# Storing q and k unsplit in a graph-network kernel with attention: parting them later on GpSimd, with fewer loads per group and another order of the last gathers

## The chip, the cores and the metric

The kernel runs on one core of one Trainium2 chip. The metric is the device time of one execution in microseconds (us). Each kernel is run several times, and the median is taken.

## The reference

Four layers of a graph network work one after the other on x (3327 nodes, 128 features) with a sparse 0/1 matrix adj (3327 x 3327). Each layer normalises x, applies a ReLU and adds its result to x.

```python
def _L1_gnn_ref(x, adj, Wq, Wk, Wv, Wo):            # layer 1: attention, 128 heads of width 8
    q = (x @ Wq.T).reshape(d, n, h)                   # d = 128 heads, n = 3327, h = 8
    k = (x @ Wk.T).reshape(d, n, h)
    v = (x @ Wv.T).reshape(d, n, h)
    a = jnp.einsum('dnh,dmh->dnm', q, k) * scale
    a = jax.nn.softmax(a + adj + adj, axis=2)
    return jnp.einsum('dnm,dmh->dnh', a, v).reshape(n, h * d) @ Wo.T

def _L3_gnn_ref(x, A, W1, b1, W2, b2, sigma, k):      # layer 3: k = 4 nearest neighbours
    z = leaky_relu(_lap_mul(A, x) @ W1 + b1)
    S = exp(-sqrt(squared distances of z + 1e-10) / (2 * sigma))
    S = jnp.where(ranks < k, S, 0.0)                  # only the 4 largest of each row stay
    return _lap_mul(S + A, x) @ W2 + b2
```

Note the head: the reshape takes d first, so a head is a run of 3327 rows of 8 numbers in the flat list of all q (or k, or v). Layer 0 multiplies twice by adj, and layer 2 is a gated recurrent cell on adj @ x. They are not touched here.

## The kernel before, in words

Nodes are cut into T = 26 tiles of 128 rows. NH = 128 heads and E = 8 numbers per head are worked on in 32 groups of four heads. The queries are cut into seven chunks of QW = 476 columns (the last has 471), the keys into 26 tiles. So attention runs over chunk c, group g and key tile t: 7 x 32 x 26 steps.

**Projection (L399 to L425).** For each row tile r, TensorE makes q, k and v in PSUM. [...]q and k are parted here into a rounded half (hi, written by ScalarE, L410) and the rest (lo, L411, on VectorE). Both halves go to DRAM: `qt` and `kt` have HL = 16 rows, eight of hi and eight of lo, and a column for each node of each head. `store` (L395) issues three transfers per tile on SyncE's queue: q, k and v (with a column of ones for the softmax's sum, EA = 9). At r = 1 the loads of the first group are issued (L421), and half of its keys are cast.

**Loads of a group (`load_heads`, L347 to L367).** For each of four heads and two halves j: one load of 16 rows of k (hi and lo) into `k_in`, and two loads of 8 rows of q, the same half twice, so that a 32-row product gives (hi + lo) x (hi + lo). Then one load of v per head. That makes 28 transfers on SyncE's queue. They are issued at t = 4 of the group before. From t = 13 on, `key_pair` (L370 to L375) casts two key tiles per step from `k_in` into tiles of fp32r on GpSimd (L374).

**Attention (L523 to L562).** The order of instructions on each engine is that of the program here (a manual schedule). A step (`scores`, L481) multiplies keys and queries for four heads (L492). The doubled adjacency is added by VectorE (L497) for three or two heads (`early` tiles), or by TensorE with a diagonal matrix (L495, `late` tiles). ScalarE takes the exponential of the `late` ones (L498), GpSimd multiplies the last head of every odd step by exp of the doubled adjacency (L500), and at every odd step ScalarE takes the exponential of the five summed parts of two steps at once (L502). Four steps later `weigh` multiplies by v (L509) and, at the last key tile, copies the result out of PSUM (L518) and stores it to `ot` (four transfers, L521). At t = 22 a stripe of the adjacency of the next chunk is loaded (`a_in`, L173) and doubled on GpSimd (L272); stripes already doubled are stored as bf16 for later layers (L479).

**Tail (L630 on).** The degree's root and several scales are made (L652 to L655, `scales`), then a loop over 26 row tiles divides by the softmax's sum, transposes and multiplies by Wo (L656 to L678). In the last layer, after the four neighbours of each node are found, `gather` (L878 to L899) fetches three rows per node by indirect transfers on GpSimd's queue (L886), five tiles per batch in one buffer `rows`, while TensorE makes the product with the adjacency; VectorE weighs and sums the rows (L894 to L899), the first of its operations, L895, being the one that frees `rows`. After all batches the output stage (L904 to L914) transposes, scales, adds and stores.

A tile of memory with one buffer can only be filled again when all its readers are done; a transfer on SyncE's queue waits on SyncE itself, with everything behind it.

Of the kernel before, what the change touches and what calls it, by code (L numbers as in the profile page):

```python
# [21 lines left out]
P = 128  # L22
# [32 lines left out]
def kernel(  # L55
# [273 lines left out]

    kt = dpool.tile([HL, GP], F32, name="kt")  # L330
# [15 lines left out]

    def load_heads(c, g):  # L347
        q0, _ = q_chunks[c]
        we = even(c)
        k_in = kq.tile([P, NP], F32, name="k_in", bufs=1)  # L350
        q4 = kq.tile([P, QW], F32R, name="q4")
        v4 = kq.tile([P, 4, T, EA], F32, name="v4")
        for i in range(4):
            n0 = (4 * g + i) * N
            for j in range(2):
                r = 32 * i + HL * j
                nc.sync.dma_start(k_in[r : r + HL], kt[:, n0 : n0 + NP])
                for k in range(2):
                    nc.sync.dma_start(
                        q4[r + E * k : r + E * k + E, :we].bitcast(F32),  # L360
                        qt[E * j : E * j + E, n0 + q0 : n0 + q0 + we],
                    )
            nc.sync.dma_start(
                v4[:, i].rearrange("p t e -> p (t e)"),
                vd[n0 : n0 + NP, :].rearrange("(p t) e -> p (t e)", t=T),
            )
        return k_in, q4, v4, []  # L367
# [9 lines left out]
    with tc.tile_pool(name="l1", bufs=1) as pool, tc.tile_pool(name="l1_ps", bufs=3, space=PSUM) as ps:  # L377
# [6 lines left out]
        for tail in (qt, kt):  # L384
            nc.gpsimd.dma_start(tail[:, N * NH :], zero)
# [12 lines left out]
        assert 3 * N + NP <= P * NH  # L398
        for r in range(T):  # L399
            kp = rows_of(r)  # L400
            lhs = hT[:, r * P : r * P + kp]
            for i, (dst, mx) in enumerate(((qt, q_max), (kt, k_max))):
# [3 lines left out]
                scale = D**-0.5 if i == 0 else 1.0  # L406
                s = st.tile([P, 2, E * NH], F32R, name="qk_st")
                full = pp[:kp].rearrange("p a b -> p (a b)")
                hi = s[:kp, 0].bitcast(F32)
                nc.scalar.activation(s[:kp, 0], full, AF.Copy, scale=scale)  # L410
                nc.vector.scalar_tensor_tensor(s[:kp, 1], full, scale, hi, op0=ALU.mult, op1=ALU.subtract)  # L411
                nc.vector.tensor_reduce(mx[:kp, r : r + 1], hi, AX.X, ALU.max, apply_absolute_value=True)
                store(dst.rearrange("e (r c) -> r e c", c=NH), s.bitcast(F32).rearrange("p a (e c) -> p (a e) c", c=NH), r, kp)
# [7 lines left out]
            if r == 1:  # L421
                first = load_heads(0, 0)
                while len(first[3]) < T // 2:
                    key_pair(first)
                e_first = [exp_of(a, 0) for a in a_first[1::2]]  # L425
# [38 lines left out]
    with tc.tile_pool(name="at_in", bufs=2) as a_pool, tc.tile_pool(name="at_p", bufs=3) as p_pool, tc.tile_pool(  # L464
# [5 lines left out]
        def load_adj(c, t):  # L470

            q0, w = q_chunks[c]
            a = a_pool.tile([P, QW], F32, name="a_in")
            load_rows(a, adjT, t, q0, w)
            return doubled(adj_pools[c % 2], a[: rows_of(t), :w], t, w)
# [47 lines left out]
        with tc.manual_schedule(engines=engines):  # L523
# [7 lines left out]
            for j, step in enumerate(steps):  # L531
# [14 lines left out]
                if t == min(4, T // 2) and more:  # L546
                    coming = load_heads(*groups[n])

                if t >= T // 2 and more:
                    key_pair(coming)  # L550
                if t == max(T - 4, 0) and c + 1 < len(q_chunks):
                    for _ in range(min(len(to_store), 1 + T // n_groups)):
                        store_adj(*to_store.pop(0))
                    while len(a_next) < T * (g + 1) // n_groups:
                        to_store.append((c + 1, len(a_next), load_adj(c + 1, len(a_next))))
                        a_next.append(to_store[-1][2])
# [73 lines left out]
    def tail(general):  # L630
# [13 lines left out]
        with ExitStack() as s:  # L644
# [7 lines left out]
            d1 = inv_sqrt(pool, deg, "d1")  # L652
            d1_in, d1_out = d1, d1
            if not general:
                d1_in, d1_out, into4, back4 = scales(pool, d1)  # L655
            with tc.tile_pool(name="lo", bufs=3) as lo, tc.tile_pool(name="lo_ps", bufs=2, space=PSUM) as ps:  # L656
                wo_s = lo.tile([NH, E, D], F32, name="wo_s", bufs=1)
                nc.gpsimd.dma_start(wo_s, wo)
                for t in range(T):
# [18 lines left out]
                    done(t + 1)  # L678

# [195 lines left out]
            cuts = list(range(0, T - T % 5, 5)) + [T]  # L875
            near_0 = 0 if general else 1

            def gather(t):  # L878
                if t not in cuts[:-1]:
                    return  # L880
                p = slice(t, cuts[cuts.index(t) + 1])
                n = p.stop - p.start
                rows = gpool.tile([P, n, 4 - near_0, D], F32, name="rows")
                for i in range(n):
                    for k in range(near_0, 4):
                        nc.gpsimd.indirect_dma_start(  # L886
                            out=rows[:, i, k - near_0, :],
                            out_offset=None,
                            in_=yd,
                            in_offset=bass.IndirectOffsetOnAxis(ap=idx[:, t + i, k : k + 1], axis=0),  # L890
# [7 lines left out]
                nc.vector.tensor_mul(w[:, :, 0], w[:, :, 0], over_t(d2_out, t, n))  # L898
                nc.vector.tensor_add(xs[:, p], xs[:, p], w[:, :, 0])  # L899

            with tc.tile_pool(name="l3_g", bufs=1) as gpool:
                agg = new_agg(pool)
                adj_product(agg, y, parts, gather)
            with tc.tile_pool(name="l3_o", bufs=3) as opool, tc.tile_pool(name="l3_ops", bufs=3, space=PSUM) as ps:  # L904
                for t0, n in quads():
                    op = ps.tile([P, 4, D], F32, name="op")
                    for j in range(n):
                        nc.tensor.transpose(op[:, j, :], slots(agg)[:, t0 + j, :], ident)  # L908
                    o = opool.tile([P, 4, D], F32, name="o")
                    nc.vector.tensor_mul(o[:, :n], op[:, :n], over_t(d2_out, t0, n))  # L910
# [137 lines left out]
```

## Time and profile before

| | |
|---|---|
| time of three runs, median | 11345.91 us (11337.25 to 11353.99) |
| the profiled execution | 11325.28 us |
| its span, mean granted clock of TensorE | 11323.4 us, 0.987 |
| TensorE busy | 10928.7 us (97%) |
| ScalarE (ACT) busy | 10214.7 us (90%) |
| VectorE (DVE) busy | 9415.9 us (83%) |
| GpSimd (POOL) busy | 5706.9 us (50%) |
| first store of the projection, first ACT instruction of attention | 387.85 us, 645.44 us |
| last gather issued | 11287.96 us |

The profile is of one execution. A busy TensorE isn't at its peak, since its matmuls are pipelined and their ends are modelled. A line of a group reads: line, engine, operation, out<-in with shapes, count | busy us in all, mean ns of one | idle time of the engine just before them, and what ended most of it. In a timeline a line begins with its start and its duration in us, and the bracket gives the engine's idle time before it. "SPq" and "POOLq" are the queues on which SyncE and GpSimd issue transfers. A wait is put down to whichever release came last by the records.

### The profile page before, as it was taken

What the parts mean: (1) busy time and instruction counts of PE and PEld (TensorE: products, weight loads), DVE (VectorE), ACT (ScalarE), POOL (GpSimd) and SP (SyncE); (2) the same over time, 40 slices, a digit from 0 to 9 for tenths busy, and PEclk for the clock granted to TensorE, in tenths of its full rate; (3) what the DMA queues carried; (4) which work ended last, traced back from release to release, by engine and by line L of the source; (5) the groups of instructions that cost most, each with busy time, mean ns of one, the idle gap of its engine ahead of it and who ended that gap; (6) DMA issues with size and microseconds to landing.
All of it is one profiled execution on the core that took longest, in us unless ns stands there. A gap on an engine that the chain in (4) does not pass through costs nothing. (4 is left out here: it accounts for less than half of the span.)

```text
span 11323.4 us, 210681 instructions
## 1 busy us (share of the span) xinstructions
PE 10928.7 (97%) x79530; PEld 3042.0 (27%) x79530; DVE 9415.9 (83%) x15475; ACT 10214.7 (90%) x9152; POOL 5706.9 (50%) x6196
## 2 busy tenths in 40 slices
PE   9789999999999999999999999999999999999896
PEld 4322222222222222222222222222222222222453
DVE  8678888888888888888888888888888888888655
ACT  0379999999999999999999999999999999999532
POOL 0135555555555555555555555555555555555203
PEclk9899999999999999999999999999999999999998
DMA  7754444443444444444444444444444443434432
GB/s 265 243 128 62 65 68 61 65 66 61 69 63 63 68 62 66 66 61 68 63 65 67 61 65 66 60 69 63 62 68 60 67 61 55 62 54 60 139 104 96
DMA packets 475902, 888.06 MB, mean 78 GB/s; under 512 B 91472, under 2 KB 422721, under 8 KB 439292
## 3 DMA queue, kind: packets, MB, share of 16 engines
q1 hardware_dynamic: 471114, 864.70, 43.3%
q8 instruction: 629, 10.31, 0.5%
q0 software_dynamic: 3760, 9.79, 0.3%
q14 instruction: 399, 3.27, 0.1%
HBM read 761.66 MB, written 112.46 MB: 77 GB/s over the span
## 5 line engine op out<-in xcount | busy, mean ns | idle before, releaser
L497 DVE TENSOR_TENSOR p<-early,a 128x476 f32<-128x476 f32 (+1 forms) x14560 | 8441.8, 646 | 1408.1 <-PE early L492 1166.6
L502 ACT ACTIVATE p<-p 128x2380 f32<-128x2380 f32 (+1 forms) x2912 | 6785.7, 2330 | 13.7 <-DVE p L497 0.9
L509 PE MATMUL acc<-p,v 128*9 128x476 f32 (+1 forms) x46592 | 5872.0, 564 | 34.7 <-POOL p L500 14.2
L500 POOL TENSOR_TENSOR p<-p,e 128x476 f32<-128x476 f32 (+1 forms) x2912 | 3537.4, 1215 | 3301.0 <-ACT p L498 3243.5
L498 ACT ACTIVATE p<-late 128x476 f32<-128x476 f32 (+1 forms) x5824 | 4552.6, 907 | 40.4 <-DMA q<-qt 20.6
L492 PE MATMUL early<-q,k 32*128 32x476 f32 (+1 forms) x14560 | 2884.4, 477 | 19.0 <-DVE p L497 19.0
L492 PE MATMUL late<-q,k 32*128 32x476 f32 (+1 forms) x8736 | 2798.9, 478 | 62.1 <-ACT p L498 36.1
L374 POOL CAST k<-k_in 128x256 fp32r<-128x256 f32 x2912 | 1944.9, 702 | 1155.2 <-DMA q<-qt 581.7
L492 PEld LDWEIGHTS late<-q,k 32*128 32x128 f32 x8736 | 1066.8, 181 | 4767.3 <-ACT p L498 3235.9
L495 PE MATMUL late<-a,two_i 128*128 128x476 bf16 (+1 forms) x5824 | 2181.1, 374 | 0.0
L492 PEld LDWEIGHTS early<-q,k 32*128 32x128 f32 x14560 | 1147.1, 181 | 24.7 <-DVE p L497 19.7
L509 PEld LDWEIGHTS acc<-p,v 128*9 128x9 f32 x46592 | 710.7, 88 | 1400.1 <-issue 1184.5
L495 PEld LDWEIGHTS <-two_i 128*128 128x128 bf16 x5824 | 556.2, 96 | 1326.3 <-issue 1326.3
L189 ACT COPY agg<-agg_ps 128x512 f32<-128x512 f32 x15 | 8.2, 591 | 484.1 <-PE agg_ps L204 290.5
L230 PE MATMUL agg_ps<-a,part 128*128 128x512 bf16 (+1 forms) x1092 | 227.1, 369 | 3.6 <-ACT agg L861 3.2
L272 POOL TENSOR_SCALAR a<-a_in 128x476 bf16<-128x476 f32 (+2 forms) x156 | 222.4, 1425 | 0.5
L410 ACT ACTIVATE qk_st<-pp 128x1024 fp32r<-128x1024 f32 (+1 forms) x52 | 53.2, 1023 | 150.2 <-DMA qt<-qk_st 67.8
L856 PE MATMUL sp<-yT,hT 128*128 128x512 f32 (+1 forms) x364 | 171.1, 611 | 12.2 <-ACT agg L861 6.3
L272 POOL TENSOR_SCALAR a<-a 128x476 bf16<-128x476 f32 (+1 forms) x26 | 36.4, 1400 | 287.8 <-DMA a<-in_adjT_dram 287.8
L204 PE MATMUL agg_ps<-a,h 128*128 128x512 f32 (+2 forms) x364 | 148.1, 570 | 26.8 <-DVE h L164 26.8
L411 DVE SCALAR_TENSOR_TENSOR qk_st<-pp,qk_st 128x1024 fp32r<-128x1024 f32 (+1 forms) x52 | 63.7, 1224 | 122.7 <-ACT qk_st L410 122.5
L518 DVE COPY o<-acc 105x476 f32<-105x476 f32 (+1 forms) x224 | 144.4, 644 | 4.6 <-PE acc L509 4.6
(231 smaller groups left out, 2438.3 us busy)
## 6 DMA issues: line engine op xcount, KB each, us to landing
k_in<-kt SPq DMA_DIRECT2D x1792, 208.0 KB
v<-vd SPq DMA_DIRECT2D x896, 117.0 KB
a<-in_adjT_dram SPq DMA_DIRECT2D x50, 1663.5 KB
a<-adj SPq DMA_DIRECT2D x78, 831.8 KB
q<-qt SPq DMA_DIRECT2D x3072, 14.9 KB
a_in<-in_adjT_dram SPq DMA_DIRECT2D x125, 238.0 KB
qt<-qk_st SPq DMA_DIRECT2D x25, 1024.0 KB
kt<-qk_st SPq DMA_DIRECT2D x25, 1024.0 KB
```

Source lines behind the costliest of these rows:

```text
L204: nc.tensor.matmul(acc[c][:, :w], lhs[:kp, t, :], a[:kp, c0 : c0 + w], start=(t == 0), stop=(t == T - 1))
L230: nc.tensor.matmul(acc[c][:, :w], part[:, t, :], a[:, c0 : c0 + w], start=(t == 0 and i == 0), stop=(t == T - 1 and i == len(parts) - 1),)
L272: nc.gpsimd.tensor_scalar(a2[:kp, :w], a, 2.0, None, op0=ALU.mult)
L374: nc.gpsimd.tensor_copy(k, slots(k_in)[:, t : t + 2, :])
L492: nc.tensor.matmul(sp[:, :we], pairs[t // 2][r, t % 2, :], q4[r, :we], start=True, stop=ways[i] != "I")
L495: nc.tensor.matmul(late[:, i - n_d, :we], two_i, a2[:, :we], start=False, stop=True)
L497: nc.vector.tensor_tensor(p8[:, places[i], :we], early[i][:, :we], a2[:, :we], op=ALU.add)
L498: nc.scalar.activation(p8[:, places[n_d] : places[3] + 1, :we], late[:, :, :we], AF.Exp)
L500: nc.gpsimd.tensor_tensor(p8[:, places[3], :we], p8[:, places[3], :we], e_a[:, :we], op=ALU.mult)
L502: nc.scalar.activation(p8[:, :5, :we], p8[:, :5, :we], AF.Exp)
L509: nc.tensor.matmul(acc[32 * i : 32 * i + EA, :w], v4[:kp, i, t, :], p8[:kp, PLACES[t % 2][i], :w], start=(t == 0), stop=(t == T - 1),)
L856: nc.tensor.matmul(sp[:, c0 : c0 + w], slots(zT)[:, t, :], z2T[:, cols], start=True, stop=False)
```

## The change

It has six parts.

1. ScalarE copies q and k as they are (plain fp32) into one staging tile, and they are stored whole in new tensors `qf` and `kf`. L411 goes. A class `Parting` loads four heads' q or k from there as [96 x 1109] (8 numbers x 12 strips), makes hi with a cast and lo with a subtraction on GpSimd in four pieces of 278 columns, and stores both halves to `kt` or `qt`. Groups 0 and 1 are parted during the projection, each later group during chunk 0.
2. `load_heads` loads q with one transfer of 16 rows instead of two of 8, reading 8 rows twice; all k and q come before the four loads of v: 20 transfers per group. The columns beyond N are set to zero by GpSimd. The first group's loads move to where its halves have been stored.
3. In chunk 0 the parting of group g + 2 is spread over the steps: k in pieces at t = 2 to 5, q at t = 6 to 9, the four stores at t = 11, and the two loads for the group after it at t = 15.
4. The stripe of adjacency is loaded at t = 6 and doubled at t = 22; the pool of `a_in` and `o4` has one buffer.
5. The degree's root and the scales are made after the Wo loop.
6. Gathers are cut 5, 5, 5, 5, 4, 2; `rows` becomes two buffers (batches 0, 1, 2 and 4 use one, 3 and 5 the other), and the last three batches stand in the output stage's loop, between the output of the row tiles (in fours, a quad) that are already gathered. GpSimd issues, in the order built: batch 0, nine of batch 3, batch 1, the rest of batch 3, batch 2, batch 4, batch 5.

The general path (a fallback that isn't run with these inputs) is adapted, which is left out here.

```diff
+    JW = 12
+    WJ = 4 * N // JW
+    W4 = -(-WJ // 4)
+    SIDES = ((kf, kt, "lo_k"), (qf, qt, "lo_q"))
+    class Parting:
+        def __init__(self, g):
+            self.g, self.hi, self.lo = g, [None] * 2, [None] * 2
+        def rows(self, ap, r):
+            return dram(ap, r * GP + 4 * self.g * N, [[GP, E], [WJ, JW], [1, WJ]])
+        def load(self, side):
+            src, _, name = SIDES[side]
+            self.lo[side] = kq.tile([E * JW, WJ], F32R, name=name, bufs=1)
+            nc.sync.dma_start(self.lo[side].bitcast(F32), self.rows(src, 0))
+        def part(self, side, i):
+            if i == 0:
+                self.hi[side] = kq.tile([E * JW, WJ], F32R, name=f"hi{side}", bufs=1)
+            p = slice(i * W4, min((i + 1) * W4, WJ))
+            hi, lo = self.hi[side][:, p], self.lo[side][:, p]
+            nc.gpsimd.tensor_copy(hi, lo.bitcast(F32))
+            nc.gpsimd.tensor_sub(lo, lo.bitcast(F32), hi.bitcast(F32))
+        def store(self, side):
+            dst = SIDES[side][1]
+            nc.sync.dma_start(self.rows(dst, 0), self.hi[side].bitcast(F32))
+            nc.sync.dma_start(self.rows(dst, E), self.lo[side].bitcast(F32))
...
     def load_heads(c, g):
+        nc.gpsimd.memset(k_in[:, N:], 0.0)
+        if w % 2:
+            nc.gpsimd.memset(q4[:, w : w + 1].bitcast(F32), 0.0)
         for i in range(4):
             n0 = (4 * g + i) * N
             for j in range(2):
                 r = 32 * i + HL * j
-                nc.sync.dma_start(k_in[r : r + HL], kt[:, n0 : n0 + NP])
-                for k in range(2):
-                    nc.sync.dma_start(
-                        q4[r + E * k : r + E * k + E, :we].bitcast(F32),
-                        qt[E * j : E * j + E, n0 + q0 : n0 + q0 + we],
-                    )
+                nc.sync.dma_start(k_in[r : r + HL, :N], kt[:, n0 : n0 + N])
+                nc.sync.dma_start(q4[r : r + HL, :w].bitcast(F32), dram(qt, E * j * GP + n0 + q0, [[0, 2], [GP, E], [1, w]]))
+        for i in range(4):
+            n0 = (4 * g + i) * N
             nc.sync.dma_start(
...
+        early = []
+        for g in range(2):
+            part = Parting(g)
+            for side in range(2):
+                early.append(lambda part=part: (part.load(0), part.load(1)) if part.lo[0] is None else None)
+                early.append(lambda part=part, side=side: [part.part(side, i) for i in range(4)] and part.store(side))
+        first, e_first = [], []
+        early.append(lambda: first.extend(load_heads(0, 0)))
+        ahead_part = Parting(2)
+        early.append(lambda: (ahead_part.load(0), ahead_part.load(1)))
+        early.append(lambda: e_first.extend(exp_of(a, 0) for a in a_first[1::2]))
+        early += [lambda: (key_pair(first), key_pair(first))] * (T // 4)
...
         for r in range(T):
-                s = st.tile([P, 2, E * NH], F32R, name="qk_st")
-                full = pp[:kp].rearrange("p a b -> p (a b)")
-                hi = s[:kp, 0].bitcast(F32)
-                nc.scalar.activation(s[:kp, 0], full, AF.Copy, scale=scale)
-                nc.vector.scalar_tensor_tensor(s[:kp, 1], full, scale, hi, op0=ALU.mult, op1=ALU.subtract)
-                nc.vector.tensor_reduce(mx[:kp, r : r + 1], hi, AX.X, ALU.max, apply_absolute_value=True)
-                store(dst.rearrange("e (r c) -> r e c", c=NH), s.bitcast(F32).rearrange("p a (e c) -> p (a e) c", c=NH), r, kp)
+                s = st.tile([P, E * NH], F32, name="qk_st")
+                nc.scalar.activation(s[:kp], pp[:kp].rearrange("p a b -> p (a b)"), AF.Copy, scale=D**-0.5 if i == 0 else 1.0)
+                nc.vector.tensor_reduce(mx[:kp, r : r + 1], s[:kp], AX.X, ALU.max, apply_absolute_value=True)
+                store(dst[:E].rearrange("e (r c) -> r e c", c=NH), s.rearrange("p (e c) -> p e c", c=NH), r, kp)
...
-            if r == 1:
-                first = load_heads(0, 0)
-                while len(first[3]) < T // 2:
-                    key_pair(first)
-                e_first = [exp_of(a, 0) for a in a_first[1::2]]
+            if r > 1 and early:
+                early.pop(0)()
...
+                if c == 0 and g + 2 < n_groups:
+                    if t == 0:
+                        parting = ahead_part
+                    for due in range(t, t + 1 if t < T - 1 else max(T, 16)):
+                        parting.at(due)
+                        if due == 15 and g + 3 < n_groups:
+                            ahead_part = Parting(g + 3)
+                            ahead_part.load(0)
+                            ahead_part.load(1)
...
-                if t == max(T - 4, 0) and c + 1 < len(q_chunks):
+                if t == min(6, T // 2) and c + 1 < len(q_chunks):
                     for _ in range(min(len(to_store), 1 + T // n_groups)):
                         store_adj(*to_store.pop(0))
-                    while len(a_next) < T * (g + 1) // n_groups:
-                        to_store.append((c + 1, len(a_next), load_adj(c + 1, len(a_next))))
-                        a_next.append(to_store[-1][2])
+                    a_in = [load_adj(c + 1, i) for i in range(len(a_next), T * (g + 1) // n_groups)]
+                if t == max(T - 4, 3) and c + 1 < len(q_chunks):
+                    for a, i, w in a_in:
+                        a_next.append(doubled(adj_pools[(c + 1) % 2], a[: rows_of(i), :w], i, w))
+                        to_store.append((c + 1, i, a_next[-1]))
...
-            cuts = list(range(0, T - T % 5, 5)) + [T]
+            cuts = [c for c in (0, 5, 10, 15, 20, 24) if c < T] + [T]
...
+                turn = i % 2 if i > 2 else 0
+                rows = gpool.tile([P, n, 4 - near_0, D], F32, name=f"rows{turn}")
...
+            n_beside = min(3, len(batches))
             with tc.tile_pool(name="l3_g", bufs=1) as gpool:
                 agg = new_agg(pool)
-                adj_product(agg, y, parts, gather)
+                adj_product(agg, y, parts, lambda t: gather(cuts.index(t)) if t in cuts[:n_beside] else None)
+                with tc.tile_pool(name="l3_o", bufs=3) as opool, tc.tile_pool(name="l3_ops", bufs=3, space=PSUM) as ps:
+                    to_write = quads()
+                    for i in range(n_beside - 1, len(batches)):
+                        if i >= n_beside:
+                            gather(i)
+                        while to_write and sum(to_write[0]) <= batches[i].stop:
```

In `Parting.at`, side 0 (k) is parted at t = 2 to 5, side 1 (q) at t = 6 to 9, and both are stored at t = 11.

## The prediction

> **What bounds the kernel now.** I read the groups of the page first, then the busy time of three stretches (projection, attention, tail), then the waits of each and the timelines around them.
>
> ```profile
> L502 ACT ACTIVATE p<-p 128x2380 f32<-128x2380 f32 (+1 forms) x2912 | 6785.7, 2330 | 13.7 <-DVE p L497 0.9
> L500 POOL TENSOR_TENSOR p<-p,e 128x476 f32<-128x476 f32 (+1 forms) x2912 | 3537.4, 1215 | 3301.0 <-ACT p L498 3243.5
> L374 POOL CAST k<-k_in 128x256 fp32r<-128x256 f32 x2912 | 1944.9, 702 | 1155.2 <-DMA q<-qt 581.7
> ...
> 380.00:655.00 275.00, 175.44 (x353) 64.37 (x352) 131.80 (x130) 87.61 (x87) 18.95 (x42) 0.84 0.93 269
> 2060.00:3480.00 1420.00, 1404.81 (x10803) 349.44 (x10795) 1220.33 (x2109) 1415.19 (x1261) 793.54 (x857) 1.00 0.43 65
> 11200.00:11324.00 124.00, 26.57 (x132) 15.17 (x129) 38.64 (x41) 1.56 (x3) 59.20 (x56) 0.61 0.26 80
> ```
>
> The last three are stretches: length, busy PE, PEld, DVE, ACT, POOL (instructions), clock, DMA share, GB/s. In attention (645 to 10590 us) ACT is busy 99.7%: it sets the pace. In the projection nothing computes much and the DMA engines are 93% busy; in the tail POOL's gathers lead. So three stages, three limits.
>
> In attention, a pair of steps takes 3.367 us between the starts of undisturbed L502, 43.78 us for 13 pairs; the mean group takes 44.44. Most of the excess is in one place: from t=19 to t=21, L502 to L502 takes 3.77 us in the mean. One group:
>
> ```profile
> 2093.81 1.21 POOL L500 TENSOR_TENSOR p<-p,e 128x476 f32<-128x476 f32 x1 [2.18 <-ACT p L498]
> 2100.28 1.33 POOL L374 CAST k<-k_in 128x256 fp32r<-128x256 f32 x2 [5.26 <-DMA q<-qt]
> 2101.58 1.20 POOL L500 TENSOR_TENSOR p<-p,e 128x476 f32<-128x476 f32 x1
> ...
> 2102.07 1.74 PE L509 MATMUL acc<-p,v 128*9 128x476 f32 x8
> ...
> 2103.32 2.65 ACT L502 ACTIVATE p<-p 128x2380 f32<-128x2380 f32 x1
> ...
> 2107.31 2.19 ACT L502 ACTIVATE p<-p 128x2380 f32<-128x2380 f32 x1
> ```
>
> POOL stands 5.26 us at the key cast of t=13, because the 28 loads of the next heads aren't all in. The L500 behind it starts at 2101.58 where the rhythm asked for 2097.2, PE's L509 is stretched from about 0.98 to 1.74, and the next L502 starts 3.99 us after its predecessor, not 3.37. Medians over groups, counted from L502(t=1): cast due 21.9, started 27.0, last k landed 25.6, L500(15) 4.4 late, L502(21) 0.40 late. Hence L500 has some 4.05 us of slack, and 0.40 x 223 = 89 us hang on this one wait.
>
> The projection is bound by its stores:
>
> ```profile
> 575.06 1.17 SPq L395 DMA_DIRECT2D qt<-qk_st  x1
> 576.32 3.92 SPq L395 DMA_DIRECT2D kt<-qk_st  x1
> 580.34 3.53 SPq L395 DMA_DIRECT2D vd<-v_st  x1
> ...
> 645.44 0.57 ACT L498 ACTIVATE p<-late 128x476 f32<-128x476 f32 x1 [20.61 <-DMA q<-qt]
> ```
>
> A tile of 128 rows every 9.02 us, and attention begins only when every store has landed. From the first store (387.85) to 645.4 are 257.6 us.
>
> **What the Trainium skill says.** "DMA: Bandwidth & Descriptors", § Why a DMA increments its semaphore by 16 and not by 1: a transfer runs on the largest number of engines, up to 16, that divides the outermost size of both sides. The packets agree: four ot stores of 9 rows leave 36 packets of data and 36 four-byte packets, one from each engine used; q loads of 8 rows leave 8. "SBUF — State Buffer", § Who interferes with whom: GpSimd reading SBUF contends with a VectorE instruction that has two SBUF inputs, not with one input. L497 reads PSUM and one SBUF tile, and L500 keeps its 1215 ns beside it. "GPSIMD Engine Reference", § 3.1: two-input elementwise work costs about 2.6 cycles an element, 2.17 ns; here 3328 elements took 7.24 us, 2.18 ns each.
>
> **The change, part by part.** 1. *Whole q and k.* A tile's q and k were 4096 packets of 512 bytes at 26.9 ns over 16 engines, 6.9 us, and v 128 packets of 4608 bytes at 0.21 us, 1.7 us. Halving the first gives 3.45 + 1.7 = 5.15, at the old ratio of pace to sum (9.02/8.6) 5.4 us; 26 tiles 140 us instead of 234.5. L411 goes from DVE (52 x 1.22 us, already beside the stores); the compute pace is then an estimated 3.6 us (three ACT copies of about a microsecond), so stores still lead. Added before attention: 6 loads and 8 stores of 96 rows, whose DRAM side has outer size 8, so 8 engines with 12 packets of about 0.19 us: 14 x 2.3 = 32 us on engines 0 to 7. The head loads cost those engines some 8 (k) + 4 (v), and q, whose source now begins with a repeat of 2, runs on two engines: 8 packets of 0.1 us (an a_in load of this shape drains in about 0.8 us) x 8 = 6.4 on engines 0 and 1. Sum 191. Bubbles: SP waits for GpSimd's parts before the first kt store (about 6 us of parts per side, half of it behind queued stores), for stored rows before the head loads, and for the last landing: 14. So about 205 against 257.6: **−52** (−35 to −75: the upper end if the parting runs on all 16 engines). Behind the waiting SP stand the next tiles' stores, nothing of ACT's that isn't waiting for them already. POOL's 16 pieces hold up the v_st memsets by at most 12 us, which four staging buffers and the store queue cover; uncovered it costs about 6 a side.
>
> 2. *20 loads per group instead of 28.* k and q alternate over 8 lanes, v follows. Bytes of k are the same: a k load holds 16 engines 0.7 to 1.7 us, in the mean 1.4. On engines 0 and 1 I count 7 x (1.2 + 0.9) + 1.2, from the first packet 6.3 after L502(1): the last k lands near 22.5 to 23.5, cast 1 to 2 us late instead of 5.1. That is inside the slack of 4.05, so the stretched pair goes: **−85** of 89. If a q load costs 1.5 us on its two engines, k lands at 26 or later and nothing is won; if k alone counts, it lands at 18. What is late next: nothing on POOL; ACT's own floor. k_in's pad memset (one short strip) and the zero column of q4 are under 0.3 us on POOL, at t=4, where it idles 2.2 us a pair.
>
> 3. *Parting in chunk 0.* 30 groups x 8 pieces, each a cast and a subtraction of 96x278. Scaled to 278 columns, the cast row (0.702 for 256) gives 0.76 and the L500 row (1.215 for 476) 0.71, up to 0.82 where a part of it is fixed: a piece is 1.42 to 1.64; I take 1.52, 365 us of POOL in all, beside ACT. L500(9) follows seven pieces, three L500 and the memset: 1.2 + 7 x 1.52 + 3.6 + 0.3 = 15.8 after L500(1), due 13.5: 2.3 late (1.6 to 3.2), inside 4.05. By t=13 the idle 2.15 us per pair has taken it back. Queued behind POOL's pieces: L500, and through it L509; SP's four stores at t=11 wait for POOL, with the lo loads of t=15 and the next head loads of t=4 behind them: 10 steps of room. **0**, from 0 to +48 (a piece of 2.0 would lose 1.6 us a group). No gain is possible here: it is added work.
>
> 4. *a_in loaded at t=6, doubled at t=22.* L272 waited 0.5 us in all: 0. With one buffer the load waits for a doubling 10 steps older: 0. If that cover failed, one group would lose at most the 2 us of a transfer.
>
> 5. *d1 and the scales after the Wo loop.* They delay its start by 3 us through PE's queue; afterwards DVE does them beside the adjacency loads: **−3** (0 to −5).
>
> 6. *Gathers.* 78 issues, and before each later batch a wait for DVE:
>
> ```profile
> 11239.89 2.08 POOL L886 DMA_INDIRECT rows<-yd,idx  x1 [4.01 <-DVE w L895]
> 11264.51 2.08 POOL L886 DMA_INDIRECT rows<-yd,idx  x1 [4.14 <-DVE w L895]
> ```
>
> Four gaps were 5.02, 5.48, 4.01, 4.14 = 18.6 us; two row buffers in turn leave one of about 5: −13.6, given back by 3 to 5 of slower issues beside DVE (2.08 instead of 0.94, as above). The last batch has 2 tiles, DVE behind it 2.9 instead of 7 us: −3. The order of DVE's instructions keeps all output work behind the last batch, so the output isn't really written in between: 0. Together **−12** (−8 to −18).
>
> Sum: −52 −85 −3 −12 = −152. The profiled execution took 11325.28 us (span 11323.4), so 11173; it lies 20.6 under the median of 11345.91, which makes **11194** in the terms of the runs.
>
> **The rivals.** *A: the head loads stay late.* Half the transfers per q, but on two engines; the cast still starts after 26. For it: 8 of the 20 transfers get slower; against: k no longer shares the engines with v. Gain 52 + 3 + 12 and some 5: 11274. *B: POOL's pieces cost 1.85 to 2.05 us,* past the slack by 0.5 to 2 us a group in chunk 0, 15 to 60 us: about 11232. For it the one pair of shapes never timed; against it the two rows above. *C: SP held by POOL and by the 8-engine transfers eats the projection's gain,* 15 left of 52: 11231. *D, slower: the pieces on POOL pass ACT's pace in chunk 0.* Past the slack, each group loses 7p − 12.4 us; all 152 are lost at 5.1 a group, p = 2.5 us, that is 1.25 an instruction, more than a 476-column L500 takes now; at p = 2.8 11194 + 30 x 7.2 = 11410. For it only that a cast and a subtraction of this shape were never timed; against it L500's steadiness beside DVE. *E: nothing changes in attention and projection alike,* 11330: the packets halve by construction, so hardly.
>
> **How the numbers follow.** Forecast 0.56 (11150 to 11215), A 0.17 (11255 to 11290), B 0.12, C 0.09, D 0.04, E 0.02. The range for 8 in 10 runs from 11150 (the upper ends, 75 + 89 + 5 + 18 = 187, give 11159, and the runs of one kernel lie 8 us to either side) to 11278, which takes in B, C and most of A; left out are D, E, a part of A and what lies below. A measurement of this kernel tells 0.2% (23 us) from no change. Faster by over 0.2%: 0.56 + 0.17 + 0.12 + 0.09 = 0.94, less 0.01 of spill; within: 0.03; slower: 0.04.
>
> **What would show it.** Right: a tile's three stores every 5.4 us, attention's first ACT some 205 us after the first store; no POOL idle above 2 us before the cast at t=13; L502 from t=19 to t=21 back to 3.37; POOL's pieces at 0.7 to 0.8 us; one DVE wait among the gathers. Wrong: packets of q in a long train on few engines with the cast waiting on k; a wait of L509 for L500 at t=9 to 11 in chunk 0; SP standing at the kt stores with idle DMA engines; gathers slowed to 2 us throughout.

## The result, and the profile after

The changed kernel takes 11188.99 us in the median (11184.25 to 11195.14, 4 runs) against 11344.12 (11337.25 to 11353.99): the ratio is 0.9864, with a 95% interval of 0.9852 to 0.9876. The prediction, 11194 in a range from 11150 to 11278, holds it. Its sum doesn't hold term by term, though. The span of the profiled execution went from 11323.4 to 11193.4 us, 130 and not 152 less, and the parts are these:

| stretch | before | after | difference | predicted |
|---|---|---|---|---|
| start to first store | 387.85 | 386.04 | -1.8 | 0 |
| first store to first exponential of attention | 257.6 | 190.2 | -67.4 | -52 |
| attention, to the end of the last big exponential | 9942.8 | 9897.0 | -45.8 | -85 |
| from there to the end | 735.2 | 720.2 | -15.0 | -15 |

The medians differ by 155 us and the spans by 130, because the profiled execution of before (11325.28) lies 19 us under the median of its kernel, and that of the changed kernel (11195.14) 6 us over its own. So the total was met because two errors of the sum cancelled in part, and because of this difference. To that extent it's luck.

The groups of the changed kernel's page, then the busy time of three stretches (length, PE, PEld, DVE, ACT, POOL with instructions, clock, DMA share, GB/s):

```profile
L557 ACT ACTIVATE p<-p 128x2380 f32<-128x2380 f32 (+1 forms) x2912 | 7568.4, 2599 | 0.4
L555 POOL TENSOR_TENSOR p<-p,e 128x476 f32<-128x476 f32 (+1 forms) x2912 | 3528.1, 1212 | 3204.3 <-ACT p L553 2998.6
L419 POOL CAST k<-k_in 128x256 fp32r<-128x256 f32 x2912 | 1936.5, 697 | 886.4 <-DMA k_in<-kt 339.4
...
380.00:580.00 200.00, 155.70 (x332) 66.06 (x331) 69.63 (x70) 83.50 (x84) 34.66 (x73) 0.86 0.88 260
2060.00:3480.00 1420.00, 1402.89 (x10855) 344.85 (x10851) 1224.19 (x2120) 1420.00 (x1267) 799.75 (x893) 1.00 0.34 65
11075.00:11193.00 118.00, 35.72 (x176) 19.49 (x173) 46.81 (x53) 1.56 (x3) 64.70 (x59) 0.66 0.33 108
```

ACT is now busy for all of the 1420 us. The third line is the surprise: POOL still stands 886 us before the key casts, 270 less than before. So the loads of k are still late, and the prediction's sign "no POOL idle above 2 us before the cast at t=13" didn't come. What changed is whether anybody suffers from it. From the waits of TensorE, first before, then after:

```profile
PEld acc L509 <- POOL p L500: 132.7, 182, 1.7
```

```profile
PEld acc L564 <- POOL p L555: 8.9, 20, 1.1
```

The columns are microseconds in all, times, longest. The wait of the product with v for GpSimd's multiplication is nearly gone. In one group of the changed kernel:

```profile
2018.17 1.21 POOL L555 TENSOR_TENSOR p<-p,e 128x476 f32<-128x476 f32 x1 [2.17 <-ACT p L553]
2023.28 1.32 POOL L419 CAST k<-k_in 128x256 fp32r<-128x256 f32 x2 [3.89 <-DMA adj<-a]
2024.56 1.20 POOL L555 TENSOR_TENSOR p<-p,e 128x476 f32<-128x476 f32 x1
```

POOL stands 3.89 us, not 5.26, and L555 starts at 2024.56 where the rhythm asks for 2021.56: 3.0 late, inside what the pipeline bears (how much that is, the experiments show). The wait's releaser, a store of the adjacency, is only the release that came last by the records; the cast reads only `k_in`. In the projection, SyncE's queue and the first instruction of attention:

```profile
528.41 1.17 SPq L440 DMA_DIRECT2D qf<-qk_st  x1
529.68 1.43 SPq L440 DMA_DIRECT2D kf<-qk_st  x1
531.22 2.26 SPq L440 DMA_DIRECT2D vd<-v_st  x1
533.57 1.17 SPq L440 DMA_DIRECT2D qf<-qk_st  x1
...
576.21 0.57 ACT L553 ACTIVATE p<-late 128x476 f32<-128x476 f32 x1 [10.22 <-DMA q<-qt]
```

A tile every 5.16 us instead of 9.02, as long as nothing but stores is in the queue. In the tail, one wait of the gathers for VectorE is left, and the evacuation of the last product (L191) and all seven quads of output come behind the last batch:

```profile
11134.22 2.07 POOL L954 DMA_INDIRECT rows<-yd,idx  x1 [4.14 <-DVE w L963]
...
11165.48 0.43 DVE L967 TENSOR_TENSOR xs<-xs,w 128x256 f32<-128x256 f32 x1
11165.82 2.21 DVE L191 COPY agg<-agg_ps 128x512 f32<-128x512 f32 x4
...
11179.64 0.42 DVE L985 TENSOR_TENSOR o<-o,xs 128x256 f32<-128x256 f32 x1
```

### The profile page after: what moved, and what is told of

Read it like the earlier page. It is cut to its first block, busy times and chain, and to the rows that moved or that the text cites. A ratio compares the mean times of both kernels' runs of the same rounds, so it can differ in the third digit from the quotient of the medians.

```text
span 11193.4 us, 209350 instructions
## 1 busy us (share of the span) xinstructions
PE 10850.5 (97%) x79530; PEld 3005.9 (27%) x79530; DVE 9343.1 (83%) x15429; ACT 10199.3 (91%) x9152; POOL 6016.3 (54%) x6964
## 5 line engine op out<-in xcount | busy, mean ns | idle before, releaser
L557 ACT ACTIVATE p<-p 128x2380 f32<-128x2380 f32 (+1 forms) x2912 | 7568.4, 2599 | 0.4
L564 PE MATMUL acc<-p,v 128*9 128x476 f32 (+1 forms) x46592 | 5748.5, 564 | 15.3 <-ACT p L557 1.4
L553 ACT ACTIVATE p<-late 128x476 f32<-128x476 f32 (+1 forms) x5824 | 5315.4, 1175 | 13.8 <-DMA q<-qt 10.2
L555 POOL TENSOR_TENSOR p<-p,e 128x476 f32<-128x476 f32 (+1 forms) x2912 | 3528.1, 1212 | 3204.3 <-ACT p L553 2998.6
L547 PE MATMUL early<-q,k 32*128 32x476 f32 (+1 forms) x14560 | 2843.6, 478 | 9.4 <-DVE p L552 9.4
L547 PEld LDWEIGHTS early<-q,k 32*128 32x128 f32 x14560 | 1113.0, 181 | 9.9 <-DVE p L552 9.9
L204 PE MATMUL agg_ps<-a,x 128*128 128x512 f32 (+2 forms) x364 | 145.3, 562 | 0.6 <-ACT x L318 0.6
L230 PEld LDWEIGHTS <-part 128*128 128x128 f16 x1092 | 108.6, 99 | 117.7 <-issue 10.3
```

Of the source, the lines that this page charges most:

```text
L204: nc.tensor.matmul(acc[c][:, :w], lhs[:kp, t, :], a[:kp, c0 : c0 + w], start=(t == 0), stop=(t == T - 1))
L230: nc.tensor.matmul(acc[c][:, :w], part[:, t, :], a[:, c0 : c0 + w], start=(t == 0 and i == 0), stop=(t == T - 1 and i == len(parts) - 1),)
L547: nc.tensor.matmul(sp[:, :we], pairs[t // 2][r, t % 2, :], q4[r, :we], start=True, stop=ways[i] != "I")
L553: nc.scalar.activation(p8[:, places[n_d] : places[3] + 1, :we], late[:, :, :we], AF.Exp)
L555: nc.gpsimd.tensor_tensor(p8[:, places[3], :we], p8[:, places[3], :we], e_a[:, :we], op=ALU.mult)
L557: nc.scalar.activation(p8[:, :5, :we], p8[:, :5, :we], AF.Exp)
```

## The experiments

Two theories of attention's gain: (1) the key cast of t=13 starts so late that L500 exceeds a slack of about 4 us, and the new order and form of the group's loads cure this alone; (2) the cure is elsewhere, such as the adjacency stripe's new place. The size is open as well. In what follows, times within a group are counted from the end of the big exponential of t=1 (L502 before, L557 after), and are medians over the groups. The prediction counted from its start: its 25.6 us for the last k of the kernel before is 23.28 here. "L500(15)" is GpSimd's multiplication of step t=15, also where the line has another number, and the "pair to t=21" is the time between the ends of the big exponentials of t=19 and t=21. A time without a range is of one execution.

**The kernel before once more.**

> The kernel before, unchanged, to see how much of its attention time differs from execution to execution. If the loss at the key cast hangs on when transfers land, the pair of steps that ends with t=19 to 21 varies: mean 3.55 to 3.70 us between ends in chunks 0 to 5, against 3.39 elsewhere, attention 9942.8 us within 10 us. If the profiled execution of before was an unusually fast one by its attention, this one shows 10 to 20 us more there; the projection (257.6 us) and the tail (735 us) stay within 2 us either way.

Measured: 11325.14 us; projection 257.6, attention 9946.6, tail 732.5. Between ends of L502, the pair to t=21 took 3.56 to 3.67 us in the mean of chunks 0 to 5, 3.69 in the last; the others 3.39. So the profile of before is repeatable to 4 us in attention; the tail differs by 2.7 us, a little more than expected. The runs beside it went from 11317 to 11352, so executions do differ more than these two profiles show; in which stretch they do, no profile caught.

**The loads alone.** The kernel before with

```diff
-                for k in range(2):
-                    nc.sync.dma_start(
-                        q4[r + E * k : r + E * k + E, :we].bitcast(F32),
-                        qt[E * j : E * j + E, n0 + q0 : n0 + q0 + we],
-                    )
+                nc.sync.dma_start(q4[r : r + HL, :we].bitcast(F32), dram(qt, E * j * GP + n0 + q0, [[0, 2], [GP, E], [1, we]]))
+        for i in range(4):
+            n0 = (4 * g + i) * N
             nc.sync.dma_start(
                 v4[:, i].rearrange("p t e -> p (t e)"),
```

> The kernel before with the loads of a group as in the changed kernel and nothing else of the change: q in one transfer of 16 rows, v after all k and q. Theory (the loss in attention is the key cast starting later than the slack of L500 allows, and the loads alone cure it): first cast 23.5 us after the end of L502(t=1) instead of 24.7, attention 9942.8 - 46 = 9897 us within 8, the whole time 11344 - 46 = 11298. Rival (the cure is the adjacency stripe moved from t=22 to t=6, or POOL's other order): 0 to -10 us. Prediction's own size: -85.

Measured: 11280.0 us (11277.9 to 11282.3), 0.9951 of before (0.9932 to 0.9971), which is 44.5 us under the runs of before beside it; attention 9897.9 us, cast at 23.55. This is the changed kernel's attention to a microsecond, with no parting and the stripe at its old place. Theory 1 stands, theory 2 falls, and 85 was too much. These four runs lie within 4.4 us, where seven of before beside them spread over 35. That may come from a wait that hangs on the landing of transfers, but it isn't shown: seven other runs of before, beside the last experiments below, lie within 6.1 us.

**Only v behind k and q, still 28 transfers.**

```diff
+        for i in range(4):
+            n0 = (4 * g + i) * N
             nc.sync.dma_start(
                 v4[:, i].rearrange("p t e -> p (t e)"),
```

> The kernel before with v's loads after all k and q, still 28 transfers with q in two of 8 rows. If what delays k is the DMA engines' time (v's share, about 1 us a load, lies before the last k; q spread over 8 engines is cheap): k lands at about 20 to 21 us after the end of L502(t=1) instead of 23.3, earlier than in the changed kernel (22.5), cast before 22.5, attention 9897 within 8. If the number of transfers in the lanes is what delays it: k lands within 0.7 us of 23.3, and attention stays above 9925.

Measured: 11272.58 us. The last k lands at 20.45 (before 23.28), the cast starts at 22.25, attention 9893.1. So the number of transfers isn't what counts; v's place in the line does.

**Only q in one transfer, v between the k.**

```diff
-                for k in range(2):
-                    nc.sync.dma_start(
-                        q4[r + E * k : r + E * k + E, :we].bitcast(F32),
-                        qt[E * j : E * j + E, n0 + q0 : n0 + q0 + we],
-                    )
+                nc.sync.dma_start(q4[r : r + HL, :we].bitcast(F32), dram(qt, E * j * GP + n0 + q0, [[0, 2], [GP, E], [1, we]]))
```

> The kernel before with q in one transfer of 16 rows, v still between the k. If q's 16 rows run on two engines with 8 packets each and so block those engines for k: k lands later than 23.3 us, by 1 to 3 us, the pair at t=19 to 21 grows by as much, attention 9942.8 + 150 to 500 us. If fewer transfers are what counts: k lands earlier, attention 9897 to 9930.

Measured: 11478.0 us, 153 more than before. The last k lands at 24.31, a microsecond later than before, the cast starts at 25.48, and the pair to t=21 takes 4.10 to 4.57 us in the means of the chunks. TensorE's waits for GpSimd (L505 and L496 of this kernel are L509 and L500 of the kernel before, where the first line had 132.7 us):

```profile
PEld acc L505 <- POOL p L496: 307.1, 216, 3.3
...
PE acc L505 <- POOL p L496: 124.2, 171, 2.5
```

Taken alone, 20 transfers instead of 28 make the kernel slower. The half of the edit that looks like the gain is the loss, and moving v pays for it. That fits the rule that the prediction cites from the Trainium skill, "DMA: Bandwidth & Descriptors" (§ Why a DMA increments its semaphore by 16 and not by 1): with two as the outer size of q's source, two engines carry it. The packets agree. Each engine used leaves one packet of four bytes, and this kernel has 65,953 of them where the kernel before has 91,041. The 25,088 fewer are 1792 q loads x 14: two packets for a merged load, where the two loads of 8 rows left sixteen.

The four kernels also give the slack. L500(15) is due at 21.72 and starts at 23.55 (v last), 24.83 (loads alone), 25.96 (before) and 26.75 (q merged); the pair to t=21 loses 0, 0 to 0.1, 0.2 to 0.4 and 0.7 to 1.2 in the means of the chunks. Group by group it's sharper (chunks 0 to 5, without the last group of each, 186 groups of a kernel). In the kernel before and in this one, no group less than 4.15 us late lost anything (72 and 4 groups); where L500(15) was over 4.3 late, lateness less loss was 4.19 to 4.26 in nine groups of ten (of 86 and 178). So the slack is 4.2 us, and beyond it the loss grows one for one. The changed kernel's L500(15) is 3.0 late in the median, and over 4.2 in 6 groups of the 186.

**Heavier parting.** The changed kernel with

```diff
             nc.gpsimd.tensor_copy(hi, lo.bitcast(F32))
+            if self.g > 1:
+                nc.gpsimd.tensor_copy(hi, lo.bitcast(F32))
+                nc.gpsimd.tensor_copy(hi, lo.bitcast(F32))
             nc.gpsimd.tensor_sub(lo, lo.bitcast(F32), hi.bitcast(F32))
```

> The changed kernel with each piece of the parting in chunk 0 made heavier by two more casts of the same columns: 0.41 us each, so a piece of 1.19 becomes 2.01 us. Theory (L500 may be late by 4.05 us, then every further microsecond goes to attention one for one): L500(9), 0.66 us late in the changed kernel, becomes 0.66 + 7 x 0.82 = 6.4 late, each group of chunk 0 loses 2.3 us, 30 groups 70 us; the prediction's formula 7p - 12.4 gives 1.7 a group, 50 us. Rival (POOL has spare time over the group, so work spread over eight steps costs nothing): chunk 0 stays at 44.13 us a group, 0. Rival (GpSimd's casts slow VectorE or ScalarE, whatever the slack): a loss spread over all of t=2 to 9, more than 70 us.

Measured: 11248.58 us. L500(9) is 6.39 us late (0.66 in the changed kernel), and chunk 0 takes 46.10 us a group instead of 44.13, 1.96 x 31 = 61 us; all of it is in one pair, that to t=15, which takes 5.50 us in 29 of the 30 groups with heavier pieces, 2.11 more than undisturbed. No other chunk moved. Lateness less loss is 4.28 us here, the same edge as at t=15. So added work on GpSimd is free up to 4.2 to 4.3 us of lateness at one L500, and beyond that it costs its full length, as in the prediction's rival D. The changed kernel was far from that edge in chunk 0, since a piece is cheaper than was estimated. Two lines on the pieces of the changed kernel:

```profile
L376 POOL TENSOR_TENSOR lo_q<-lo_q,hi 96x278 fp32r<-96x278 f32 x96 | 74.6, 778 | 7.2
...
L375 POOL CAST hi<-lo_k 96x278 fp32r<-96x278 f32 x96 | 39.6, 413 | 5.4 <-DMA kf<-qk_st 3.3 <-DMA lo_k<-kf 2.1
```

**More engines for the same transfers.** The changed kernel with

```diff
-            return dram(ap, r * GP + 4 * self.g * N, [[GP, E], [WJ, JW], [1, WJ]])
+            return dram(ap, r * GP + 4 * self.g * N, [[WJ, JW], [step * GP, E], [1, WJ]])
...
-            nc.sync.dma_start(self.rows(dst, 0), self.hi[side].bitcast(F32))
-            nc.sync.dma_start(self.rows(dst, E), self.lo[side].bitcast(F32))
+            step = 2 - side
+            nc.sync.dma_start(self.rows(dst, 0, step), self.hi[side].bitcast(F32))
+            nc.sync.dma_start(self.rows(dst, (1, E)[side], step), self.lo[side].bitcast(F32))
...
-                nc.sync.dma_start(q4[r : r + HL, :w].bitcast(F32), dram(qt, E * j * GP + n0 + q0, [[0, 2], [GP, E], [1, w]]))
+                nc.sync.dma_start(q4[r : r + HL, :w].bitcast(F32), dram(qt, E * j * GP + n0 + q0, [[GP, E], [0, 2], [1, w]]))
```

> The changed kernel with its transfers laid out for more DMA engines, the work the same: the parting's loads and stores with the 12 strips outermost (12 engines instead of 8), the halves of k interleaved in DRAM, so that q is loaded as 8 rows, each twice (8 engines instead of 2). If engines 0 to 7 bound the projection: first store to first exponential 190.2 - 5 to 12 us; if the parting's transfers hide beside the other stores: within 2 us of 190.2. In both, the last k lands 1.5 to 2.5 us earlier than 22.5 after the end of L557(t=1), the cast with it, and attention changes by less than 6 us, since the cast was already inside the slack.

Measured: 11188.53 us, projection 185.5. Six kernels with the changed kernel's layout and stores took between 188.2 and 190.2 in the projection, and the second kernel of the new layout (the last one below) took 186.6. So this is 2 to 5 us less, between the two outcomes that were expected, and engines 0 to 7 held the projection up by that little. The last k lands at 21.11 instead of 22.49, 1.4 earlier and not the 1.5 to 2.5 expected. The cast doesn't follow by as much: it starts at 22.83 instead of 23.48, 1.7 us behind the last k where the changed kernel has 1.0 (what fills that time wasn't tried). Attention is 9895.0. For q this is the opposite test to merging its loads: just as many transfers, on eight engines instead of two (with the halves of k interleaved for it), and k is there earlier. The packets of four bytes grow by 11,520, that is 1792 q loads x 6 and 192 of the parting's transfers x 4.

**Output really between the gathers.** The changed kernel with the last product, gathers and output under a manual schedule for VectorE:

```diff
             n_beside = min(3, len(batches))
+            with tc.manual_schedule(engines={mybir.EngineType.DVE}):
...
```

> The changed kernel with VectorE's instructions of the last product, gathers and output in the order in which the program writes them, so that the evacuation of the sums and the output of the first six quads come before the last batch. If the output stage after the last batch is what ends the kernel: the time from the end of attention to the end goes from 720.2 to 708 to 712 us (the last batch is followed by one quad instead of an evacuation and seven). If contention with GpSimd's issues eats it: 716 to 721.

Measured: 11175.06 us; 705.6 from the end of attention, 14.6 less than the changed kernel, and 11 to 14 less than five other runs with its tail (716.8 to 719.8). That is as much as was expected or more. The end of VectorE's work:

```profile
11158.83 0.43 DVE L967 TENSOR_TENSOR xs<-xs,w 128x256 f32<-128x256 f32 x1
11159.18 0.42 DVE L985 TENSOR_TENSOR o<-op,d_out 128x256 f32<-128x256 f32 x1
11159.63 0.42 DVE L986 TENSOR_TENSOR o<-o,xs 128x256 f32<-128x256 f32 x1
```

One quad follows the last batch. From the last gather's issue to the last output instruction it takes 6.6 us, in the changed kernel 19.8.

**The tail of before on the changed kernel.** The gathers and the output stage as in the kernel before, and the four lines of `d1` ahead of the Wo loop.

> The changed kernel with the tail of the kernel before: the gathers cut in fives behind one buffer, and the degree's scales ahead of the Wo loop. Sum of both by the prediction: -3 for the scales, -12 for the gathers, so this is 15 us slower than the changed kernel, all after the end of attention. By the two traces I expect the scales to be worth less (0.5 us at the first gather, the loop's own 2 us being lost again on the way) and the gathers 12 to first and last issue, 2 to 3 behind it.

Measured: 11201.98 us; 734.4 from the end of attention, 14 more than the changed kernel. From first to last gather 122.1 us against 110.1; the first gather is at 577.1 after attention, in the changed kernel at 577.0. So the gathers are worth 12, what lies behind them 2, and the scales nothing: the Wo loop starts 3.1 us earlier in the changed kernel (11.8 against 14.9) and ends at the same time (104.7 against 104.8); the lead is lost around the 17th to 20th tile. What takes it there wasn't tried.

**Is ScalarE the floor?** The changed kernel with

```diff
-                nc.scalar.activation(p8[:, :5, :we], p8[:, :5, :we], AF.Exp)
+                nc.scalar.activation(p8[:, :4, :we], p8[:, :4, :we], AF.Exp)
```

> The changed kernel with the exponential of each pair of steps (L557) over four of its five parts: one head of every even step is left without its exponential, 476 columns less for ScalarE per pair. Question: is the floor of 3.388 us a pair, which all undisturbed groups of both kernels keep, ScalarE's own? The two widths of chunk, 476 and 472, differ by 32 columns and 0.027 us a pair, 0.84 ns a column, so 476 columns are worth 0.40 us. If ScalarE alone sets it and the next engine is far off: 2.99 us a pair, attention -1165 us. If TensorE (busy 98.9% of this stretch in the kernel before) stands close behind: 3.25 to 3.37 a pair, attention -50 to -400. If ScalarE doesn't set it: within 10 us of 9895.

Measured: 10958.64 us, attention 9665.9, a pair 3.29 us. The same stretch as above:

```profile
2060.00:3480.00 1420.00, 1416.37 (x11111) 348.88 (x11115) 1252.34 (x2170) 1329.42 (x1296) 819.00 (x918) 1.00 0.35 66
```

ACT falls to 94%, PE rises to 99.7%. So ScalarE sets the floor of 3.39 us a pair in the changed kernel and, since the floor is the same there, in the kernel before. The next limit stands 0.1 us a pair behind it, since 0.40 us less work on ScalarE won no more; by its busy share that is TensorE. The pair to t=21 grew to 3.50 to 3.64 again: at a faster pace the same loads are late once more.

**Every tile of q and k stored twice.**

```diff
                 store(dst[:E].rearrange("e (r c) -> r e c", c=NH), s.rearrange("p (e c) -> p e c", c=NH), r, kp)
+                store(again[i][:E].rearrange("e (r c) -> r e c", c=NH), s.rearrange("p (e c) -> p e c", c=NH), r, kp)
```

> The changed kernel with q and k of every tile stored a second time, to tensors that nobody reads. If the stores' packets set the projection's pace after the change as they did before (2048 packets of 512 bytes more per tile, 26.9 ns each over 16 engines, 3.44 us): a tile every 8.6 us instead of 5.16, first store to first exponential 190 + 89 = 279 within 8. If computing or the waits on GpSimd's parts set it: 190 to 230.

Measured: 11286.31 us, projection 282.0. Two tiles of SyncE's queue:

```profile
599.32 1.18 SPq L441 DMA_DIRECT2D qf<-qk_st  x1
...
608.25 1.18 SPq L441 DMA_DIRECT2D qf<-qk_st  x1
```

A tile every 8.9 us, 3.8 more than 5.16 where packets alone give 3.44. With as many packets of q and k per tile as the kernel before, this kernel has its pace too (9.02), without L411. So the stores set the projection's pace in both kernels. SyncE's own time to issue them isn't the limit: in the changed kernel the first store of q, of k and of v, before the queue had filled, took 0.42, 0.40 and 0.38 us to issue, where the later ones take 1.17, 1.43 and 2.26.

**A better version.** First the changed kernel again on the same chip.

> The changed kernel again, to be compared with the next on the same chip: 11175 to 11195, 0.987 to 0.988 of the kernel before.

Measured: 11192.16 us (11191.71 to 11195.02), 0.9874 of before (0.9857 to 0.9890). Then the two edits above (more engines, VectorE's order) with

```diff
-                turn = i % 2 if i > 2 else 0
+                turn = (0, 1, 2, 0, 1, 2)[i]
```

> The changed kernel with three things that the runs so far point to: the parting's transfers on 12 engines and q on 8 (projection -4), VectorE's output instructions in program order (-14 behind the last gather), and three buffers for the gathered rows in turn, so that no batch waits for VectorE (another -3 to -6: the gap of 5 us goes, each batch's three slow issues stay). Sum -21 to -24 against the changed kernel: 11155 to 11170. If the order of outputs and the gathers' issues get in each other's way: -15.

Measured: 11168.81 us (11164.42 to 11170.10), 0.9851 of before (0.9835 to 0.9868), 23 us under the changed kernel beside it: 20.5 in the tail, 1.8 in the projection. Of the 20.5, 14 are behind the last gather and 3 in the gathers (106.3 us without a gap, 109.2 beside it). The other 3.4 lie ahead of the first gather (573.7 us after attention, 577.1 beside it), where none of the three edits was meant to change anything; what saved them is open.

## Why the prediction was right or wrong, step by step

1. *Whole q and k: right, the size 15 us short (-67.4 against -52).* Stores bound the stage before and after. The pace of undisturbed tiles was 5.16 and not 5.4 us, 6 us over 26 tiles. What isn't stores came to 190.2 - 26 x 5.16 = 56 us, where 65 were counted: SyncE stood about 3 us at the first kt store and 1 at that of group 1, since queued stores filled most of the time of GpSimd's pieces. The head loads took their 20 us. Running the parting on few engines cost 2 to 5.

2. *Fewer transfers per group: the mechanism right, both numbers wrong (-45.8 against -85).* The step that failed was the size of the loss, "0.40 x 223 = 89 us hang on this one wait". It was read from start to start of L502. The records of ScalarE overlap, and a big exponential recorded as 2.19 us after a stall lengthens to 2.65 within a group: its start creeps ahead of its end, into the instruction before it. From the group of before that the prediction showed, the two instructions ahead of its pair of L502 and the L502 behind it:

```profile
2099.95 2.63 ACT L502 ACTIVATE p<-p 128x2380 f32<-128x2380 f32 x1
2102.03 1.86 ACT L498 ACTIVATE p<-late 128x476 f32<-128x476 f32 x2
...
2110.69 2.19 ACT L502 ACTIVATE p<-p 128x2380 f32<-128x2380 f32 x1
```

The L498 starts at 2102.03, before the L502 ahead of it ends. With the two L502 that the prediction showed, the ends lie at 2102.58, 2105.97, 2109.50 and 2112.88: 3.39, 3.53, 3.38 apart. The stalled pair lost 0.14 us, though its starts are 3.99 apart. By ends, the floor is 3.388 us and not 3.367, and a group without a wait takes 44.04 us. Against the changed kernel's groups, those of before took 0.12 to 0.22 us more in chunks 0 to 5 and 0.39 in the last, 47 us in all: no more than that was there to be won.

The second number was the landing of k. It came 0.8 us earlier (22.49 against 23.28), not 2 to 3, and the cast 1.2 earlier: moving v gave 2.8 us, and q's slow transfer took 2 of them back. The stretched pair went all the same, since L500(15) came from 4.2 late, at the edge of the slack, to 3.0. Rival A, the loads staying late, was right about this mechanism and wrong in the end by about a microsecond of slack. The slack itself, 4.05 predicted, was measured as 4.2 to 4.3.

3. *Parting in chunk 0: right at 0.* The piece was over-priced: 1.19 us, not 1.52. L500(9) was 0.66 us late instead of 2.3. Rivals B and D needed 1.85 and more; the heavier piece of 2.01 cost 61 us, 2.11 a group, where the formula 7p - 12.4 gives 1.67 x 30 = 50.

4. *The stripe at t=6: 0, as said;* the loads alone, with the stripe at t=22, reach the same attention.

5. *The scales: -3 predicted, 0 measured.* The earlier start of the loop was there; the step that failed was that its lead would last. It was gone by the loop's end, and what took it is open.

6. *Gathers: right.* -12 from first to last issue where 9 to 11 were worked out, and 2 to 3 behind them as forecast. That output wouldn't come between the gathers was right as well; making it so is worth 11 to 15 us more.

Rival C (SyncE held by GpSimd's parts) had its waits, 4 us in all instead of 37.

## What to carry to other kernels

Measure the pace of a saturated engine from end to end: where its records overlap, a stall seen from start to start contains the slack that had built up before it. Before merging small transfers, look at the outermost sizes: fewer transfers on fewer engines can be slower, and what helped here was putting what isn't urgent behind what is. A wait that is still long may have stopped costing; ask who is late at its end, and by how much more than they can bear.

## What the runs showed of the hardware that was not expected

A cast of 96 partitions x 278 columns in a row took 0.413 us on GpSimd, while the key cast of 128 x 256 columns, whose source takes every 26th word, took 0.697; a subtraction of 278 columns took 0.778. Whether the stride makes the difference wasn't tried. In the loads of 16 rows of k, a packet of 13.3 KB took 1.36 us in the mean in the kernel before and 1.25 in the changed kernel, while packets of that size in loads over 128 partitions took 0.58 in the kernel before. With q on eight engines, where all of k landed earlier, the packets of k took longer, 1.55. So the time of one packet didn't tell how soon the loads were done.
